# Constants later, Newton steps in another slot, and eight instead of twelve transfers an image, in a four-layer pre-activation kernel

## The chip, the cores and the metric

The kernel runs on one core of a Trainium2 chip. The metric is the device time of one execution in microseconds, lower is better. The engines go by the names of the profile: PE is TensorE's matrix product and PEld its weight load, DVE is VectorE, ACT is ScalarE, POOL is GpSimd, and SP is SyncE, which in this kernel does little but issue transfers (DMAs); its queue is shown as SPq. Each engine runs its own instructions in order; semaphores order the engines among each other.

## The reference

The input x has 4 images of 32x32 positions and 16 channels. Four layers each add a function of the normalized input:

```python
def _gn(v, G=8, eps=1e-5):                    # group norm over positions and channel pairs
    B_, H_, W_, C_ = v.shape
    g = v.reshape(B_, H_, W_, G, C_ // G)
    m = jnp.mean(g, axis=(1, 2, 4), keepdims=True)
    s = jnp.var(g, axis=(1, 2, 4), keepdims=True)
    return ((g - m) / jnp.sqrt(s + eps)).reshape(v.shape)

x = x + conv(_gn(x), L0_M, L0_W, L0_G)
x = x + conv(_gn(x), L1_M, L1_W, L1_G)
x = x + interval(_gn(x), W0, b0, W1, b1, W2, b2)
x = x + conv(_gn(x), L3_M, L3_Wp, L3_G)
```

In a convolution layer, with i, j an output position, c a channel and y, x an input position,

```python
first   = einsum('ijyx,byxc->bijc', M, v)
shifted = 3x3 convolution of v with the weights G[i, j], which differ for every i, j
diff    = relu(v - shifted)                   # one 32x32 plane for every b, i, j, c
second  = einsum('ijyx,bijyxc->bijc', W, diff)
return first - second
```

The interval layer takes a running maximum and a running minimum over all intervals (i, j), runs two steps of the form max over k of sigmoid(f[i,k] Wf + r[k,j] Wr + b), the second on the first's result, and ends with a linear map and a sigmoid.

Here 1024 output positions times 4 images times 16 channels each need a plane of 1024 values for every convolution layer, and this is nearly the whole work.

## The kernel before

**Tiling.** The 4 images are two groups g of 2 images b. Each convolution layer of each group is a phase, six in all: (g 0, layer 0), (g 1, layer 0), (g 0, layer 1) and so on; the kernel counts its convolution layers 0, 1, 2, the last being the reference's fourth. The interval layer belongs to the preparation of layer 2. A phase has 8 chunks t of 128 output positions, and a chunk has 32 steps, one for each output channel f and image b. So there are 6x8x32, 1536 steps. A step makes 128 planes in one pair of PSUM banks, of which there are four:

- first_part: PE multiplies the weights WL by ib and WU by ia (eight matmuls, L663 by way of products), and ACT scales the result in place (L699).
- second_part, issued one step later: PE adds the products of iyz and im9 (six matmuls), and DVE reads the pair, takes the minimum with 0, multiplies by the chunk's W (tile WT) and sums (L716, output junk). That frees the pair for the step four later.

The inputs ia, ib, iyz and im9 of a group are made in its preparation from the normalized images: split (L275 ff) separates each value into a high part and a rest (upper at L204 on DVE, the subtraction L281 on POOL, a scaling on ACT) and writes both to a tile temp; place (L291 ff) copies quarters of temp to other partitions of ia and ib by DMA, twelve an image (eight of 32x496 values for ia at L299, four of 32x2x512 for ib at L301); difference makes iyz. In the first chunk, which works with plain inputs for the first eight channels, temp is a part of the tile called first, and DVE does the subtraction.

**The weights' cycle.** A unit is the weights of 4 channels, used for 8 steps. The generator prep_parts (L221 ff) prepares the units one after the other; conv_layer advances it once a step, so a unit's preparation takes the 8 steps of another unit. Its slots, in order of steps:

- slot 1: DVE takes the high part, upper_w (L204);
- slot 2: ACT, W9 (L176);
- slot 3: ACT (L237) and POOL (L238, L239);
- slot 4: ACT (L241) and POOL (L242, two L244, two L246);
- slot 5: POOL subtracts the picked identity from the next unit's raw weights (L215);
- slot 6: nothing;
- slot 7: SP issues two transfers of parts to the other half of the partitions (L252) and the load of raw weights two units ahead (L111);
- slot 0: nothing.

**Everything else.** All other work of a phase (the preparation of the next group: norm, interval layer, image copies, split, place, and the product sum first_terms) is one long generator, behind(phase). conv_layer advances it after a step's matmuls have been issued: a yield of n waits n steps, a yield of IDLE waits for a slot in which the weights' cycle allows it (slots 1, 5, 6, 7, 0), a yield of CALM for one of slots 6, 7, 0. So a number in a yield decides in which slot of the cycle, and so between which instructions of POOL, DVE, ACT and SP, all the following work stands.

The order on each engine is the order in which the program issues, and nothing is reordered. SP issues all the transfers in that order too. The transfers of SP pass through eight semaphores in turn, so that a transfer is issued only when the one eight before it has landed.

**What the change and the prediction touch.** group_norm (L334 ff) sums over positions on DVE, transposes, sums again (by totals, with pauses of gap steps), makes mean, difference and squares on POOL (L366 ff), sums the squares in the same way, and takes the inverse root (inverse_root, three DVE instructions from L320 and thirteen POOL instructions, L326 to L331, three Newton steps) and the product with it (L376). The interval layer calls it with the name i0 or i1 and a gap of 2. constants (L462 ff) loads the interval layer's weights wv and bv, masks them and builds the small block matrices f0, f1, f2, r0, r1 by POOL products (L476). It is called once, in the first phase, in behind. step (L598 ff) is one of the interval layer's two steps; it ends in a sigmoid (L630) and four transfers of the hidden state s into the tile tables (L632), which left reads next on PE (L573). rest_of_start (L905 ff) prepares group 0 in the first chunk and ends in its norm, c00.

Of the kernel before, what the change touches and what calls it, by code (L numbers as in the profile page):

```python
# [8 lines left out]
F32 = mybir.dt.float32  # L9
F32R = mybir.dt.float32r  # L10
# [5 lines left out]
P = 128  # L16
B, H, C = 4, 32, 16
NG = 2
GB = B // NG
# [5 lines left out]
HW = H // 2  # L25
WP = HW + 2
PITCH = H * WP
NH = H * HW
RUN = (H - 1) * WP + HW
LAST = (H - 1) * HW  # L30
TAPS = ((0, 1, 2, 3), (6, 7, 4, 5))
TEMP = 2 * 2 * GB * NH
# [13 lines left out]
def net_kernel(ctx: ExitStack, tc: tile.TileContext, x, xq, xi, convs, iv_w, iv_b, out):  # L46
# [26 lines left out]
    nc = tc.nc  # L73
# [6 lines left out]
    big = ctx.enter_context(tc.tile_pool(name="big", bufs=1))  # L80
# [19 lines left out]
    CALM = -1  # L100
# [32 lines left out]
    first = big.tile([P, 8192], F32, tag="big", name="first")  # L133
    used = PLAIN * 3 * FU * P
# [60 lines left out]
    QUARTERS = [(slice(64 * h, 64 * h + 32), slice(64 * h + 32, 64 * h + 64)) for h in range(2)]  # L195
# [73 lines left out]
        halve_rest(units[u][3][:, at:to], raws[u][:, 2, at:to], low_p)  # L269

    def halves(temp, b):
        v = temp.rearrange("p (k s b n) -> p k s b n", k=2, s=2, b=GB)
        return v[:, 0, :, b], v[:, 1, :, b]

    def split(eng, g, b, temp, name, pause=IDLE):  # L275
# [14 lines left out]

    def place(g, b, temp):  # L291

        ty, tz = (v.bitcast(F32) for v in halves(temp, b))
        da, db = (v[g].bitcast(F32)[:, :, b] for v in (ia, ib))
        for h, (lo, hi) in enumerate(QUARTERS):
            for s in range(2):
                at = HW if s == h else 0
                for to, src in ((lo, ty), (hi, tz)):
                    nc.sync.dma_start(da[to, s, :LAST], src[lo, s, at : at + LAST])  # L299
            for to, src in ((lo, ty), (hi, tz)):  # L300
                nc.sync.dma_start(db[to], src[hi])  # L301
        yield 1


# [26 lines left out]
            nc.gpsimd.tensor_tensor(y, y, t, ALU.mult)  # L331
        return y

    def group_norm(g, name, dst, gap):  # L334


        def sums(src):
            nc.vector.tensor_reduce(
                part[:, : GC // 2], src.rearrange("p t (g s) -> p g t s", s=2), axis=AX.XY, op=ALU.add
            )  # L340

        def totals(name):

            turned = work.tile([P, 32], F32, tag="turned", name=f"turned_{name}")
            nc.vector.transpose(turned, part)
            by_quarter = work.tile([32, 4], F32, tag="by_quarter", name=f"by_quarter_{name}")
            for q in range(4):
                nc.vector.tensor_reduce(
                    by_quarter[:, q : q + 1], turned[32 * q : 32 * q + 32], axis=AX.X, op=ALU.add
                )  # L350
            yield gap
            total = work.tile([P, 32], F32, tag="total", name=f"total_{name}")
            for q in range(4):
                nc.vector.tensor_reduce(
                    total[32 * q : 32 * q + 32, 0:1], by_quarter, axis=AX.X, op=ALU.add
                )
            yield gap
            whole = work.tile([P, 32], F32, tag="whole", name=f"whole_{name}")
            nc.vector.transpose(whole, total[:, 0:1].to_broadcast([P, 32]))
            return whole[:, : GC // 2]  # L360

        sums(X[g])
        yield gap
        m = yield from totals(f"m{name}")
        mean = work.tile([P, GC // 2], F32, tag="mean", name=f"mean_{name}")
        nc.gpsimd.tensor_scalar_mul(mean, m, 1.0 / (2 * NP))  # L366
        xc = work.tile([P, NT, GC], F32, tag="xc", name=f"xc_{name}")
        nc.gpsimd.tensor_tensor(pair_view(xc), pair_view(X[g]), spread(mean), ALU.subtract)
        sq = work.tile([P, NT, GC], F32, tag="sq", name=f"sq_{name}")
        nc.gpsimd.tensor_tensor(sq, xc, xc, ALU.mult)  # L370
        yield 4
        sums(sq)
        yield gap
        v = yield from totals(f"v{name}")
        rstd = inverse_root(v, name)
        nc.gpsimd.tensor_tensor(pair_view(dst), pair_view(xc), spread(rstd), ALU.mult)  # L376
        yield 6

    xns = {}
    part = const.tile([P, 32], F32, name="part")  # L380
# [2 lines left out]
    def before_conv(g, layer):  # L383
        xn = work.tile([P, NT, GC], F32, tag="xn", bufs=2, name=f"xn_{g}_{layer}")
        xns[g] = xn
        yield from group_norm(g, f"c{g}{layer}", xn, 1 if layer == 2 else 4)

        nc.vector.transpose(  # L390
            xt[g][:, :, 1 : 1 + H], xn
        )
        inner = xs[g][:, :, WP : WP + H * WP].rearrange("p h (t r n) -> p h r t n", r=ROWS, n=WP)
        for r in range(ROWS):
            for h in range(2):
                nc.sync.dma_start(
                    inner[:, h, r], xt[g][GC * r : GC * (r + 1), :, HW * h : HW * h + WP]
                )
        yield 2
        xsv = xs[g].rearrange("(b c) h n -> c h b n", b=GB)  # L400
        for slot, row, tap in [
            (slot, row, tap) for slot in range(2) for row, tap in enumerate(TAPS[slot])
        ] + [(2, row, 8) for row in range(4)]:
            for h in range(2):
                off = tap // 3 * WP + tap % 3
                r0 = 64 * h + C * row
                nc.sync.dma_start(
                    raw[r0 : r0 + C, slot ^ h if slot < 2 else 2, :, :RUN], xsv[:, h, :, off : off + RUN]
                )
            yield 1  # L410
        yield 6 if layer == 2 else 12
        temp = big.tile([P, 8192], F32R, tag="big", name=f"temp_{g}{layer}")[:, :TEMP]
        for b in range(GB):
            yield from split(nc.gpsimd, g, b, temp, f"{g}{layer}")
            yield IDLE
            halve(image(im9[g][:, b], HW), image(raw[:, 2, b], WP), low_x)
            yield from place(g, b, temp)
            for s in range(2):
                difference(nc.gpsimd, g, b, s, temp)
            yield 1  # L420
            halve_rest(image(im9[g][:, b], HW), image(raw[:, 2, b], WP), low_x)
            yield 4
# [39 lines left out]
    def constants():  # L462
        nc.sync.dma_start(wv, iv_w)
        nc.sync.dma_start(bv, iv_b)
        mask2 = const.tile([P, GB], F32, name="mask2")
        nc.vector.tensor_reduce(
            mask2, ident.rearrange("p (s b c) -> p b s c", b=GB, c=C), axis=AX.XY, op=ALU.add
        )

        for at in (GC, 3 * GC):  # L470
            nc.gpsimd.tensor_scalar_mul(mask2[at : at + GC], mask2[at : at + GC], -1.0)
        yield 2

        def blocks(dst, k, mask, n, p0=0):
            p = dst.shape[0]
            nc.gpsimd.tensor_tensor(  # L476
                dst,
                wv[p0 : p0 + p, k, :].unsqueeze(1).to_broadcast([p, n, C]),
                mask[p0 : p0 + p].unsqueeze(2).to_broadcast([p, n, C]),
                ALU.mult,  # L480
            )

        nc.gpsimd.memset(rt, 0.0)
        yield 1


        for k, hidden, name in ((0, None, "f0"), (3, 2, "f1"), (6, 5, "f2")):
            n = 64 if hidden is None else 96
            t = const.tile([n, GB, C], F32, name=name)
            blocks(t[:64], k, mask2, GB)  # L490
            if hidden is not None:
                blocks(t[64:], hidden, mask2, GB, 64)
            iv[name] = t.rearrange("p k c -> p (k c)")
            yield 1
        for k, name in ((1, "r0"), (4, "r1")):
            t = const.tile([P, NQ * GB, C], F32, name=name)
            for q in range(NQ):
                blocks(t[:, q * GB : (q + 1) * GB, :], k, mask2, GB)
            iv[name] = t.rearrange("p k c -> p (k c)")
            yield 1  # L500
    def interval_layer(g):

        R = 2 * GC
        xi = ivp.tile([P, NT, GC], F32, tag="xi", name=f"xi_{g}")
        tables = big.tile([P, 8192], F32, tag="big", name=f"tables_{g}")
        n = H * H
        one, other, resets = (tables[:R, k * n : (k + 1) * n] for k in range(3))
        at = 3 * n
# [14 lines left out]
        yield 1  # L523
        nc.gpsimd.memset(r[:R, :, 0:1], 0.0)
        nc.gpsimd.memset(r[:R, H:], 0.0)
        yield from group_norm(g, f"i{g}", xi, 2)

        raw = one[:GC].rearrange("p (j t r) -> p r t j", j=H, r=ROWS)
        for row in range(ROWS):
# [68 lines left out]
        def step(name, ftp, bias):  # L598
# [26 lines left out]
                maxima(i, 0)  # L625
                yield 4
            maxima(QI - 2, 1)
            yield 3
            yield IDLE
            nc.scalar.activation(s, s, AF.Sigmoid, bias=bias)  # L630
            for q in range(NQ):
                nc.sync.dma_start(r[R:, QI * q : QI * (q + 1), :], s[GC * q : GC * (q + 1)])  # L632
            yield 4

        yield from right_side("r0", iv["r0"])
        ftp = left("l0", iv["f0"])
# [132 lines left out]
    def behind(phase):  # L769
        g, layer = phases[phase]  # L770
        if phase == 0:
            yield from rest_of_start()
            nc.sync.dma_start(X[1], x[1])
            zeros(1)
            yield 1
            yield from constants()
        if phase + 1 < len(phases):
            g1, layer1 = phases[phase + 1]
# [126 lines left out]
    def rest_of_start():  # L905
# [12 lines left out]
        halve_rest(image(im9[0][:, 1], HW), image(raw[:, 2, 1], WP), low_x)  # L918
        prep_plain_rest(1)
        yield 2  # L920
        temp = first.bitcast(F32R)[:, used : used + TEMP]
        for b in range(GB):
            yield from split(nc.vector, 0, b, temp, "00", 1)
            yield from place(0, b, temp)
# [4 lines left out]
        nc.vector.memset(part, 0.0)  # L929
        zeros(0)  # L930
        xns[0] = work.tile([P, NT, GC], F32, tag="xn", bufs=2, name="xn_00")
        yield from group_norm(0, "c00", xns[0], 4)

    parts = prep_parts()
    for phase in range(len(phases)):
# [80 lines left out]
```

## Time and profile before

| What | Value |
|---|---|
| Median of three runs | 2475.79 us (2475.51 to 2481.12) |
| The profiled execution | 2478.91 us |
| Its span (first to last instruction) | 2477.1 us |
| Granted TensorE clock | 1.000 of full speed |
| Matmuls of a step (L663), mean of one | 379 to 388 ns, 14 a step, pipelined |
| ACT on a step (L699) | 1008 ns |
| DVE on a step (L716) | 1224 ns, and 83 ns for the sum's read |
| POOL on a unit (L238, L239, L242; L244, L246 twice each; L215) | 1300, 1302, 1300; 609, 613; 1052 ns |
| Bytes moved | 366.92 MB, 148 GB/s |
| Transfers for ia and ib after the first preparation | 80 of 62 KB and 40 of 128 KB; landing after 5.6 and 4.4 us (medians) |
| Load of raw weights | 190 of 768 KB, 7.1 us (median) |
| SP's queue at an ia issue, waiting for a raw load to land | 26.1 us in all, 10 times |

In the groups of instructions, a row gives the source line, the engine, the operation, the tile written and the tiles read, the shape and the count; then the busy time, the mean of one, and the idle time of that engine just before these instructions with what ended most of it. In the timeline each row begins with its start and its duration in microseconds; a bracket at its end gives the engine's idle time before it and what released it. A table of waits sums such idle times by what was waited for. In the chain of waits, read from the last instruction back, each row is start, duration and what it was; PE's rows stand for matmuls, DMA's for the time from issue to landing.

An engine's idle time costs nothing unless it reaches the engine that sets the pace. A step that takes longer than the others shows as a late start of its first matmul in the timeline.

### The profile page before, as it was taken

How to read it: one execution, taken by the hardware profiler on the slowest of the kernel's cores; microseconds unless marked ns; L12 is line 12 of the kernel's file. 1: busy time of each engine (PE TensorE's matmuls, PEld its weight loads, DVE VectorE, ACT ScalarE, POOL GpSimd, SP SyncE). 2: the span in 40 equal slices, each digit the busy share in tenths (PEclk: the TensorE clock that was granted, in tenths of full speed). 3: DMA queues.
4: the chain of work that ended last, by engine and by line, in shares of the span. 5: the costliest groups of instructions: out<-in, count | busy, mean ns of one | idle time of the engine just before them, and what ended most of it. 6: DMA issues, size and time to landing. Idle time of an engine off the chain costs nothing. (4 is left out here: it accounts for less than half of the span.)

```text
span 2477.1 us, 58166 instructions
## 1 busy us (share of the span) xinstructions
PE 2457.9 (99%) x21906; PEld 2072.9 (84%) x21906; DVE 2077.0 (84%) x3637; ACT 1871.4 (76%) x2159; POOL 1589.7 (64%) x1857
## 2 busy tenths in 40 slices
PE   8999999999999999999999999999999999999999
PEld 5998888888888888888888898888889888888887
DVE  9888878888888888878888888888888888788887
ACT  3778767787777778767777777777777787677776
POOL 4767545676565667555567776776777675555552
PEclk9999999999999999999999999999999999999999
DMA  6457654475444467644454454674445476554442
GB/s 198 128 156 191 188 144 134 131 195 149 135 142 137 137 168 194 190 112 136 137 145 129 126 142 132 174 171 130 129 135 141 119 197 186 154 148 137 137 137 54
DMA packets 97674, 366.92 MB, mean 148 GB/s; under 512 B 26480, under 2 KB 31472, under 8 KB 97392
## 3 DMA queue, kind: packets, MB, share of 16 engines
q1 hardware_dynamic: 96832, 362.79, 53.5%
q8 instruction: 172, 2.82, 0.5%
q14 instruction: 110, 0.90, 0.1%
q10 hardware_dynamic: 432, 0.39, 0.0%
q0 software_dynamic: 128, 0.02, 0.0%
HBM read 199.78 MB, written 1.02 MB: 81 GB/s over the span
## 5 line engine op out<-in xcount | busy, mean ns | idle before, releaser
L716 DVE SCALAR_TENSOR_TENSOR junk<-pc,WT 128x1024 f32<-128x1024 f32 x1536 | 1879.6, 1224 | 353.5 <-PE pc L663 303.8
L699 ACT ACTIVATE pc<-pc 128x1024 f32<-128x1024 f32 x1520 | 1532.2, 1008 | 563.8 <-PE pc L663 530.4
L663 PE MATMUL pc<-ib,parts 64*128 64x512 f32 x6080 | 950.2, 388 | 4.3 <-DVE junk L716 3.0
L663 PE MATMUL pc<-iyz,parts 64*128 64x512 f32 x6080 | 947.2, 387 | 2.3 <-ACT pc L699 1.6
L663 PE MATMUL pc<-ia,parts 64*128 64x496 f32 x6080 | 924.8, 379 | 0.0
L663 PEld LDWEIGHTS pc<-ib,parts 64*128 64x128 f32 x6080 | 582.4, 184 | 109.8 <-DVE junk L716 9.6
L663 PEld LDWEIGHTS pc<-ia,parts 64*128 64x128 f32 x6080 | 585.4, 184 | 106.0
L663 PEld LDWEIGHTS pc<-iyz,parts 64*128 64x128 f32 x6080 | 583.5, 184 | 92.6 <-ACT pc L699 7.3
L663 PE MATMUL pc<-im,W 64*128 64x496 f32 x3072 | 603.2, 384 | 0.0
L238 POOL TENSOR_TENSOR parts<-raw,upper_w 128x512 fp32r<-128x512 f32 x190 | 247.0, 1300 | 497.6 <-DVE upper_w L204 413.1
L663 PEld LDWEIGHTS pc<-im,W 64*128 64x128 f32 x3072 | 296.6, 184 | 56.9 <-issue 3.4
L244 POOL CAST parts<-parts 32x512 fp32r<-32x512 f32 x380 | 231.6, 609 | 39.3 <-ACT parts L241 20.8
L242 POOL TENSOR_TENSOR parts<-parts 128x512 fp32r<-128x512 f32 x190 | 247.0, 1300 | 1.6 <-ACT parts L237 1.5
L246 POOL CAST parts<-upper_w 32x512 fp32r<-32x512 f32 x380 | 233.1, 613 | 22.8
L239 POOL TENSOR_TENSOR W<-W,raw 128x512 fp32r<-128x512 f32 x190 | 247.4, 1302 | 0.4 <-ACT W L176 0.3
L215 POOL TENSOR_TENSOR raw<-raw,ident 128x512 f32<-128x512 f32 x190 | 199.8, 1052 | 73.7 <-DMA raw<-in_g 45.8
L176 ACT ACTIVATE W<-raw,low_w 128x512 fp32r<-128x512 f32 x190 | 136.2, 717 | 1.7 <-DMA raw<-in_g 1.6
L716 DVE DVE_READ_ACCUMULATOR junk<-pc,WT 128x1 f32 x1536 | 127.9, 83 | 0.0
L237 ACT ACTIVATE parts<-upper_w 128x512 fp32r<-128x512 f32 x190 | 118.9, 626 | 7.7 <-DVE upper_w L204 7.5
L241 ACT CAST parts<-upper_w 128x512 fp32r<-128x512 f32 x190 | 116.4, 613 | 0.0
L731 POOL TENSOR_SCALAR acc<-acc 128x32 f32<-128x32 f32 x40 | 15.6, 391 | 136.8 <-DVE junk L716 134.7
L204 DVE TENSOR_SCALAR upper_w<-raw 128x512 int32<-128x512 int32 x190 | 82.4, 433 | 19.0 <-POOL raw L215 18.6
(152 smaller groups left out, 470.4 us busy)
## 6 DMA issues: line engine op xcount, KB each, us to landing
raw<-in_g SPq DMA_DIRECT2D x190, 768.0 KB, 7.1
parts<-parts SPq DMA_DIRECT2D x380, 384.0 KB, 5.0
WT<-in_w SPq DMA_DIRECT2D x48, 512.0 KB, 4.7
MT<-in_mt SPq DMA_DIRECT2D x24, 512.0 KB, 7.3
raw<-xs SPq DMA_DIRECT2D x120, 71.8 KB, 4.1
ib<-temp SPq DMA_DIRECT2D x40, 128.0 KB, 4.4
ia<-temp SPq DMA_DIRECT2D x80, 62.0 KB, 5.6
ib<-first SPq DMA_DIRECT2D x8, 128.0 KB, 2.4
```

Of the source, the lines that this page charges most:

```text
L176: nc.scalar.activation(dst, src, AF.Copy, scale=mask[:, 1:2])
L215: eng.tensor_tensor(raws[u][:, s, at:to], raws[u][:, s, at:to], pick[s][:, f0 + at : f0 + to].unsqueeze(2).to_broadcast([P, to - at, P]), ...
L237: nc.scalar.activation(WD, high, AF.Copy, scale=-EPS)
L238: nc.gpsimd.tensor_tensor(WL, w8, high, ALU.subtract)
L239: nc.gpsimd.tensor_tensor(W9, W9.bitcast(F32), src[:, 2], ALU.add)
L241: nc.scalar.copy(WU, high)
L242: nc.gpsimd.tensor_tensor(WD, WD.bitcast(F32), WL.bitcast(F32), ALU.add)
L244: nc.gpsimd.tensor_copy(WU[hi], WL[lo].bitcast(F32))
L246: nc.gpsimd.tensor_copy(WL[lo], high[hi])
L663: nc.tensor.matmul(ps[:, h, at : at + n], lhsT=w[r], rhs=v[r] if n == NH else v[r][:, :n], start=first and k == 0, stop=k == len(pairs) - ...
L699: nc.scalar.activation(ps, ps, AF.Copy, scale=1.0 + EPS)
L716: nc.vector.scalar_tensor_tensor(junk, ps.rearrange("p h n -> p (h n)"), 0.0, chunks[n], op0=ALU.min, op1=ALU.mult, accum_out=accs[phase][ ...
```

## The change

Five edits, most of them in the pauses of behind.

1. place sends ib first (four transfers as before), then ia in four transfers of 32x2x496 instead of eight of 32x496: both halves s of a quarter lie in temp at a fixed distance, 16 values (half an image row) more or less than the distance of the two planes, and one access pattern with that pitch covers them. To form the pattern, temp is no longer cut to TEMP columns when it is made, and halves cuts it.
2. group_norm gets a pause before inverse_root and the number of steps after it as arguments. The norm of group 0 in the first chunk (c00) gets a CALM pause there.
3. The interval norm (i0, i1) gets gap 1 instead of 2, the CALM pause, and 4 steps behind it instead of 6.
4. constants starts 6 steps after the zeros instead of 1, has 9 steps instead of 2 after the loads, 2 instead of 1 after clearing rt, and one step for each of the four blocks of r0 and r1. What comes after it in the first phase starts 24 steps later (three units).
5. In step, the wait before the sigmoid is 2 steps instead of 3, and the wait after its transfers is 5 instead of 4.

```diff
     def halves(temp, b):
-        v = temp.rearrange("p (k s b n) -> p k s b n", k=2, s=2, b=GB)
+        v = temp[:, :TEMP].rearrange("p (k s b n) -> p k s b n", k=2, s=2, b=GB)
         return v[:, 0, :, b], v[:, 1, :, b]
...
     def place(g, b, temp):
 
-        ty, tz = (v.bitcast(F32) for v in halves(temp, b))
+        parts = halves(temp.bitcast(F32)[:, :TEMP], b)
         da, db = (v[g].bitcast(F32)[:, :, b] for v in (ia, ib))
+        for lo, hi in QUARTERS:
+            for to, src in zip((lo, hi), parts):
+                nc.sync.dma_start(db[to], src[hi])
         for h, (lo, hi) in enumerate(QUARTERS):
-            for s in range(2):
-                at = HW if s == h else 0
-                for to, src in ((lo, ty), (hi, tz)):
-                    nc.sync.dma_start(da[to, s, :LAST], src[lo, s, at : at + LAST])
-            for to, src in ((lo, ty), (hi, tz)):
-                nc.sync.dma_start(db[to], src[hi])
+            for k, to in enumerate((lo, hi)):
+                at = (2 * k * GB + b) * NH + HW * (1 - h)
+                pitch = GB * NH + HW * (2 * h - 1)
+                src = temp.bitcast(F32)[lo, at : at + 2 * pitch].rearrange("p (s n) -> p s n", s=2)
+                nc.sync.dma_start(da[to, :, :LAST], src[:, :, :LAST])
         yield 1
...
-    def group_norm(g, name, dst, gap):
+    def group_norm(g, name, dst, gap, pause=None, behind=6):
...
         sums(sq)
         yield gap
         v = yield from totals(f"v{name}")
+        if pause is not None:
+            yield pause
         rstd = inverse_root(v, name)
         nc.gpsimd.tensor_tensor(pair_view(dst), pair_view(xc), spread(rstd), ALU.mult)
-        yield 6
+        yield behind
...
-        temp = big.tile([P, 8192], F32R, tag="big", name=f"temp_{g}{layer}")[:, :TEMP]
+        temp = big.tile([P, 8192], F32R, tag="big", name=f"temp_{g}{layer}")
...
         for at in (GC, 3 * GC):
             nc.gpsimd.tensor_scalar_mul(mask2[at : at + GC], mask2[at : at + GC], -1.0)
-        yield 2
+        yield 9
...
         nc.gpsimd.memset(rt, 0.0)
-        yield 1
+        yield 2
...
             for q in range(NQ):
                 blocks(t[:, q * GB : (q + 1) * GB, :], k, mask2, GB)
+                yield 1
             iv[name] = t.rearrange("p k c -> p (k c)")
-            yield 1
...
-        yield from group_norm(g, f"i{g}", xi, 2)
+        yield from group_norm(g, f"i{g}", xi, 1, CALM, 4)
...
             maxima(QI - 2, 1)
-            yield 3
+            yield 2
             yield IDLE
             nc.scalar.activation(s, s, AF.Sigmoid, bias=bias)
             for q in range(NQ):
                 nc.sync.dma_start(r[R:, QI * q : QI * (q + 1), :], s[GC * q : GC * (q + 1)])
-            yield 4
+            yield 5
...
             zeros(1)
-            yield 1
+            yield 6
             yield from constants()
...
-        temp = first.bitcast(F32R)[:, used : used + TEMP]
+        temp = first.bitcast(F32R)[:, used:]
...
-        yield from group_norm(0, "c00", xns[0], 4)
+        yield from group_norm(0, "c00", xns[0], 4, CALM)
```

## The prediction

> **What bounds the kernel now.** I began with the page's engine row, the clock row and the two costliest groups.
>
> ```profile
> PE 2457.9 (99%) x21906; PEld 2072.9 (84%) x21906; DVE 2077.0 (84%) x3637; ACT 1871.4 (76%) x2159; POOL 1589.7 (64%) x1857
> ...
> PEclk9999999999999999999999999999999999999999
> ...
> L716 DVE SCALAR_TENSOR_TENSOR junk<-pc,WT 128x1024 f32<-128x1024 f32 x1536 | 1879.6, 1224 | 353.5 <-PE pc L663 303.8
> ```
>
> PE is busy 99% of the span at full clock, and DVE's main instruction mostly waits for PE. So TensorE's products set the pace, and the change removes none of them. In the timeline the first product of consecutive steps starts at 794.65, 796.22, 797.79 us: a step is 1.567 us, and 1536 of them are the time. The periods above that pace, summed over all steps after the twentieth, are 46.2 us. Only these can be won, and a stall counts only if it reaches a PE row. I therefore listed the long periods in the timeline and looked for those whose cause the edit touches. Three numbers serve below. A PSUM buffer comes back when DVE has read it; in steady steps DVE ends 1.65 us before PE needs that buffer, so **DVE may be 1.65 us late for nothing**, and it catches up 0.2 us a step (1.567 less 1.23+0.08 for L716, less its other work). A weight unit takes 8 steps, 12.54 us; POOL's part of it, from L238 to the end of L215, takes 7.6 us and starts right after upper_w (L204), so with some 0.5 us of starts **POOL may be 4.4 us late** before the next L204 waits. L204 stands in order in front of L716, which is how POOL's lateness reaches PE.
>
> **The change part by part.** Times over pace are sums of periods less 1.567.
>
> *Interval norm (L326 to L376, twice).*
>
> ```profile
> 1276.82 1.29 POOL L238 TENSOR_TENSOR parts<-raw,upper_w 128x512 fp32r<-128x512 f32 x1
> ...
> 1284.45 0.43 DVE L204 TENSOR_SCALAR upper_w<-raw 128x512 int32<-128x512 int32 x1 [2.49 <-POOL raw L215]
> ...
> 1286.07 0.73 PE L663 MATMUL pc<-ib,parts 64*128 64x512 f32 x4 [0.80 <-DVE junk L716]
> ```
>
> The Newton steps sit in slot 1 of the unit, ahead of L238; they last 1272.12 to 1276.86, so L238 starts at 1276.82 instead of about 1270.3, 6.5 late against 4.4. L204 waits 2.49, PE 0.80, and DVE needs many steps to recover: from 1272 to 1303 the periods stand 2.01 us over pace, and 2.01 again for the second group (1684 to 1715). The edit puts the Newton steps three steps earlier, in slot 6, where POOL is free: 1272.1−3×1.567 is 1267.4 to 1272.1, L238 follows at about 1272.3, its L215 ends at 1279.9, and L204 is due at 1282: 2 us to spare. What stays is ACT's 1.06 us multiplication in that stretch (L533, 1295.16), for which I leave 0.3. Gain 1.7 twice, **3.4**. The price is crowding: pauses of 1 instead of 2 put DVE's reductions and transposes into consecutive steps. No row shows this norm so. The nearest is the layer-2 convolution norm, which has pauses of 1: at 1550 DVE was 1.89 late, 0.07 short of the limit, and the steps 1554 to 1558 lost 0.36. By adding the reductions to the DVE rows of this stretch I get at most 1.45, below 1.65. I take 0, between 0 and 0.4 each. Below nothing is excluded, as no DVE work goes. The mean's three POOL instructions fall behind the copies L246, and their unit's L215 ends at 1256.1 for an L204 at 1256.9: hidden, by 0.8 plus DVE's 1.65.
>
> *First norm and constants.*
>
> ```profile
> 108.19 0.23 POOL L476 TENSOR_TENSOR f<-wv,mask 64x32 f32<-64x32 f32 x1 [2.46 <-DMA wv<-in_iv_w]
> ...
> 115.74 0.50 PE L663 MATMUL pc<-ib,parts 64*128 64x512 f32 x2 [1.06 <-DVE junk L716]
> ```
>
> The first norm's Newton steps (87.81 to 92.55) delay L238 in the same way; L204 waits 1.80 at 100.14, and 95 to 108 is 0.68 over pace. They move five steps, to slot 6, the place argued above: gain 0.68. Then the first constant block waits 2.46 on POOL for a load of wv, with L242 to L215 queued behind it; L204 waits 2.41, PE 1.06, and 108 to 131 is 1.48 over pace. The edit loads wv ten steps later and uses it another eleven steps (17 us) after, where an issue at 103.20 landed at 108.12; and the thirteen small blocks (0.23 to 0.26 each) come one or two a step. Gain 1.48. Everything behind them (mask, X[1]'s load, the norm of image group 1, its transfers, the MT loads, the first product sum from step 195 to 219) moves by 24 steps, three whole units, so each instruction and DMA meets the same slot of a unit and the same free queue as before. The first terms' matmuls only run later (7.27 us over pace before and after). The two mask products now stand before L238 behind a DVE reduction: L238 is 3.65 late of 4.4, so 0, or 0.3 if that sum is off. Together **2.2**.
>
> *Eight transfers an image (L291 ff).*
>
> ```profile
> 1625.18 5.42 SPq L299 DMA_DIRECT2D ia<-temp  x4
> 1630.64 1.29 SPq L301 DMA_DIRECT2D ib<-temp  x2
> 1632.12 1.16 SPq L252 DMA_DIRECT2D parts<-parts  x2
> 1633.69 0.82 SPq L111 DMA_DIRECT2D raw<-in_g  x1
> ...
> 1643.95 1.04 POOL L215 TENSOR_TENSOR raw<-raw,ident 128x512 f32<-128x512 f32 x1 [7.36 <-DMA raw<-in_g]
> ```
>
> SP issues everything in order, and each transfer waits for the one eight before it. The eighth after the raw of 1617.60 (landed 1628.34) is issued at 1628.36, and four more follow it before parts and raw can go. So this raw goes out at 1633.69 and lands at 1643.82; POOL waits 7.36 for it and PE, at 1645.59, 1.21; 1638 to 1653 is 1.94 over pace. With eight transfers the eighth is the image's last, so parts follow at about 1628.95 instead of 1632.12: 3.2 us earlier, more than PE's whole stall. Gain 1.94. In the first chunk it is the same: the blocked eighth is issued at 46.11, the last ib at 48.63 lands at 51.01, and PE waits 0.96 for it (51.14); the period is 1.25 long. With ib first, its four transfers land by 47.6 and ia by about 48.5, before PE asks at 50.18. Gain 1.25. The other four preparations show no PE stall at this place, so the earlier issue is worth nothing there. Together **3.2**.
>
> A rule speaks against this. The Trainium skill, "DMA: Bandwidth & Descriptors", section "Issuing engines are not separate DMA queues", says that the time a sequencer takes to initiate a DMA is usually small beside the DMA. The bytes stay 1008 KB an image (8×62+4×128 before, 4×124+4×128 after), so by the rule alone this part is worth 0 and my sum drops to 6.9. The trace has twelve issues at 0.54 to 0.63 an image, seven us, against a landing of 5.6 (ia, the page's median), and a queue behind them: I go by the rows.
>
> The part adds a wait: image 1's first split (L281, POOL) writes a tile that image 0's ia transfers now read whole, so it waits for them. Queued behind it are L238 to L215. In the five preparations after the first, the transfer at the same count landed at 542.35, 943.97 and so on, and L281 started at 545.73, 947.23, 1615.56, 2027.35: margins 3.4, 3.3, 2.2 and 2.0 us. I cost it at 0.
>
> *Sigmoid and its four transfers one step earlier.*
>
> ```profile
> 1935.62 5.67 DMA tables<-s_b
> 1941.29 0.14 issue
> 1941.43 1.07 PE ps_l L573 x8
> ```
>
> This is the chain of waits: PE waits 0.73 here and 0.61 at 1529 for the hidden state's transfers. One step is 1.567, so they land about 1.0 us before PE asks. The matmuls remain. The four issues (2.65 us) now go ahead of parts and raw, which leave 4.3 us later (1520.53 to about 1524.8); that raw would land at about 1533.4 and L215 takes it at 1534.36: hidden by 1 us, else 0.3. Gain 0.61+0.73, **1.3**.
>
> **Sum.** 3.4+2.2+3.2+1.3 is 10.1 us against the profiled execution, 2478.91 (span 2477.1 and 1.81 around it): 2468.8. The median of the runs shown is 3.1 lower, with runs from 2475.51 to 2481.12, so some stalls of the profile are not in every run. The instruction-timed ones (norms and constants, 5.56) I take in full, of the transfer-timed ones (4.53) some seven tenths: 8.8. **Forecast 2467.0**, chance 0.60.
>
> **Rivals.**
>
> 1. *Transfer stalls are taken over* (0.20). Where PE no longer waits for ib, s_b or this raw, the next of that queue is late. For it: every raw around images takes 9 to 10 us. Against: the eighth transfer then is the last before parts. Only norms and constants pay: 2475.8−5.6 is 2470.2.
> 2. *DVE crowding* (0.12). Pauses of 1 push DVE beyond 1.65 twice. For it: the row at 1550. Then D's 3.4 goes and 0.36 to 1 is paid each time: 8.8−3.4−0.8 is 4.6, 2471.2.
> 3. *Slower: image 1's split waits on POOL* (0.08). Place: L281, five preparations. If ia's landing took the 10.1 us of raw in this stretch instead of 2 to 2.5, at 1611.93 it would end at 1622.0, 6.3 after L281's start. Decisive from 2.0 (margin) plus 1.8 (POOL's slack left after L281's 2.58) plus 1.65: some 5.5 us late; with weight loads as long as that, DVE's recovery at 0.2 a step doubles the direct 0.8 to 3 us, five times 3.4 against 8.8: 2484. Against it: merged ia is 124 KB, near ib's 128 KB, which lands in 4.4 (page).
>
> **Numbers.** What a measurement can tell from no change is 0.3%, 7.4 us, so below 2468.4 is faster. The forecast's 0.60 and a third of rival 1 make 0.66; the rest of rivals 1 and 2 are within, 0.28; slower is most of rival 3, 0.06. The range: low 2463.5 is the lowest run less the whole 10.1 and 1.9 more, one stall of 1638's size saved elsewhere; high 2473.5 takes in rivals 1 and 2 with the unknown costs (0.4 twice, 0.3 twice) and leaves out rival 3.
>
> **What will show it.** L204's waits at POOL L215 near 100, 114, 1284 and 1696 gone; no PE idle at 51, 1286, 1529, 1645, 1941; SP's raw near 1630; L281 of image 1 without an idle before it. Idle before L238 for a DMA, or DVE's L716 more than 1.65 us behind near 1250 to 1275, would prove me wrong.

## The result and the profile after

| | Before | After |
|---|---|---|
| Median, six runs each | 2477.49 us (2475.51 to 2482.97) | 2469.16 us (2468.21 to 2470.02) |
| The profiled execution, and its span | 2478.91, 2477.1 | 2470.02, 2468.3 |
| Sum of the periods over pace after step twenty | 46.20 us | 37.70 us |

The ratio is 0.9963, with a 95% interval of 0.995 to 0.9976: 8.3 us less by the medians, 8.9 between the two profiled executions. From here on lines of place, group_norm and what follows are 2 to 4 higher than before: L328 is the Newton steps' first row, L380 the product after them, L480 a constant block, L667 the products, L720 DVE on a step.

First the pages: DVE's upper_w of the kernel before, and then of the changed kernel the engines, the clock and the same row.

```profile
L204 DVE TENSOR_SCALAR upper_w<-raw 128x512 int32<-128x512 int32 x190 | 82.4, 433 | 19.0 <-POOL raw L215 18.6
```

```profile
PE 2454.2 (99%) x21906; PEld 2039.1 (83%) x21906; DVE 2077.4 (84%) x3637; ACT 1871.7 (76%) x2159; POOL 1587.7 (64%) x1857
...
PEclk9999999999999999999999999999999999999999
...
L204 DVE TENSOR_SCALAR upper_w<-raw 128x512 int32<-128x512 int32 x190 | 82.4, 434 | 8.1 <-POOL raw L215 7.6
```

PE still sets the pace at full clock, and nothing of its work is gone. DVE's waiting for POOL's L215 fell by 11 us. The timeline of the changed kernel at the first interval norm (start, duration):

```profile
1268.67 0.67 POOL L380 TENSOR_TENSOR xi<-xc_i,root_y_i 128x256 f32<-128x256 f32 x1
1269.31 1.29 POOL L238 TENSOR_TENSOR parts<-raw,upper_w 128x512 fp32r<-128x512 f32 x1
...
1275.87 1.04 POOL L215 TENSOR_TENSOR raw<-raw,ident 128x512 f32<-128x512 f32 x1
...
1280.14 0.43 DVE L204 TENSOR_SCALAR upper_w<-raw 128x512 int32<-128x512 int32 x1
```

L215 ends 3.2 us before L204, where it had been the cause of a 2.49 us wait. The constants, in the timeline:

```profile
131.37 1.30 POOL L480 TENSOR_TENSOR f<-wv,mask 64x32 f32<-64x32 f32 x5
```

No bracket: the wait of 2.46 us for wv is gone. And SP's queue where the second image of group 0 is placed for layer 2:

```profile
1611.86 1.26 SPq L111 DMA_DIRECT2D raw<-in_g  x1
1613.21 3.48 SPq L297 DMA_DIRECT2D ib<-temp  x4
1616.73 6.18 SPq L303 DMA_DIRECT2D ia<-temp  x4
1624.14 2.27 SPq L252 DMA_DIRECT2D parts<-parts  x2
1626.52 0.54 SPq L111 DMA_DIRECT2D raw<-in_g  x1
...
1632.67 1.04 POOL L215 TENSOR_TENSOR raw<-raw,ident 128x512 f32<-128x512 f32 x1
```

The raw weights land before L215 needs them. The sigmoid's transfers, at the place where the chain of waits stood before:

```profile
1926.08 2.44 SPq L636 DMA_DIRECT2D tables<-s_b  x4
1928.63 1.17 SPq L252 DMA_DIRECT2D parts<-parts  x2
...
1933.03 0.66 PE L577 MATMUL ps_l<-tables,f 96*32 96x264 f32 x8
```

PE's left product has no idle time before it now.

Not everything went down. The chain of waits of the changed kernel leaves PE once in chunk 30, in a place where before had no loss:

```profile
1563.23 9.25 DMA raw<-in_g
1572.49 0.30 SPq L411
...
1576.53 7.24 DMA parts<-parts
1583.77 0.04 issue
1583.81 6.35 PE pc L667 x48
```

A raw load took 9.25 us. The eighth transfer after it, one of the image's copies, could not be issued before it had landed, the parts transfers stood behind those copies, and PE waited for parts.

The periods over pace by place, in us, of both kernels (chunks of 32 steps; half a chunk where it says so):

| Place | What the change does there | Before | After | Predicted change |
|---|---|---|---|---|
| chunk 0, second half | eight transfers | 1.25 | 0.47 | -1.25 |
| chunk 1, second half | first norm, constants | 2.03 | 0.00 | -2.16 |
| chunks 3 (second half) and 4 | moved by 24 steps | 0.41 | 0.86 | 0 |
| chunks 24 and 25, middle | interval norm | 2.00 | 0.30 | -1.7 |
| chunks 27 and 35, end | first sigmoid of a layer | 4.00 | 3.54 | 0 |
| chunks 29 and 37 | second sigmoid | 4.54 | 2.99 | -1.34 |
| chunk 30, second half | nothing | 0.00 | 1.44 | 0 |
| chunk 31, second half | eight transfers | 1.94 | 0.00 | -1.94 |
| chunks 32 and 33, middle | interval norm | 2.01 | 0.30 | -1.7 |

### The profile page after: what moved, and what is told of

Its sections match the earlier page's. It is cut to its first block, busy times and chain, and to the rows that moved or that the text cites. A ratio compares the mean times of both kernels' runs of the same rounds, so it can differ in the third digit from the quotient of the medians.

```text
span 2468.3 us, 58094 instructions
## 1 busy us (share of the span) xinstructions
PE 2454.2 (99%) x21906; PEld 2039.1 (83%) x21906; DVE 2077.4 (84%) x3637; ACT 1871.7 (76%) x2159; POOL 1587.7 (64%) x1857
## 4 chain that ended last, share of the span: by engine, by line
PE 97%; DMA 1%; ACT 1%; issue 0%; DVE 0%; SPq 0%; ACTq 0%; DVEq 0%
PE pc L667 95%; PE pf L443 1%; DMA raw<-in_g 1%; ACT pc L703 1%; DMA first<-in_g 0%; DMA parts<-parts 0%; DVE junk L720 0%; ACT temp L285 0%; PE ps_l L577 0%; SPq L400 0%; SPq L411 0%; PE ps_r L592 0%; SPq L252 0%; DVE W L179 0%; ACT im L176 0%
## 5 line engine op out<-in xcount | busy, mean ns | idle before, releaser
L720 DVE SCALAR_TENSOR_TENSOR junk<-pc,WT 128x1024 f32<-128x1024 f32 x1536 | 1879.7, 1224 | 355.6 <-PE pc L667 305.1
L667 PE MATMUL pc<-ib,parts 64*128 64x512 f32 x6080 | 944.4, 387 | 0.7 <-DMA parts<-parts 0.7
L667 PE MATMUL pc<-iyz,parts 64*128 64x512 f32 x6080 | 942.0, 387 | 1.3 <-ACT pc L703 0.7
L667 PE MATMUL pc<-ia,parts 64*128 64x496 f32 x6080 | 919.9, 379 | 0.0
L667 PEld LDWEIGHTS pc<-ia,parts 64*128 64x128 f32 x6080 | 575.3, 184 | 115.9
L667 PEld LDWEIGHTS pc<-ib,parts 64*128 64x128 f32 x6080 | 573.5, 184 | 113.2 <-issue 4.9
L667 PEld LDWEIGHTS pc<-iyz,parts 64*128 64x128 f32 x6080 | 574.1, 184 | 100.4 <-ACT pc L703 5.6
L667 PE MATMUL pc<-im,W 64*128 64x496 f32 x3072 | 598.4, 384 | 0.0
L238 POOL TENSOR_TENSOR parts<-raw,upper_w 128x512 fp32r<-128x512 f32 x190 | 247.2, 1301 | 525.1 <-DVE upper_w L204 443.9
L667 PEld LDWEIGHTS pc<-im,W 64*128 64x128 f32 x3072 | 291.6, 184 | 61.9 <-issue 3.4
L246 POOL CAST parts<-upper_w 32x512 fp32r<-32x512 f32 x380 | 233.1, 613 | 22.8
L215 POOL TENSOR_TENSOR raw<-raw,ident 128x512 f32<-128x512 f32 x190 | 198.0, 1042 | 57.1 <-DMA raw<-in_g 24.5
L176 ACT ACTIVATE W<-raw,low_w 128x512 fp32r<-128x512 f32 x190 | 136.2, 717 | 0.3 <-DMA raw<-in_g 0.2
L720 DVE DVE_READ_ACCUMULATOR junk<-pc,WT 128x1 f32 x1536 | 128.0, 83 | 0.0
L204 DVE TENSOR_SCALAR upper_w<-raw 128x512 int32<-128x512 int32 x190 | 82.4, 434 | 8.1 <-POOL raw L215 7.6
```

The costliest lines, as they stand in the source:

```text
L176: nc.scalar.activation(dst, src, AF.Copy, scale=mask[:, 1:2])
L215: eng.tensor_tensor(raws[u][:, s, at:to], raws[u][:, s, at:to], pick[s][:, f0 + at : f0 + to].unsqueeze(2).to_broadcast([P, to - at, P]), ...
L238: nc.gpsimd.tensor_tensor(WL, w8, high, ALU.subtract)
L246: nc.gpsimd.tensor_copy(WL[lo], high[hi])
L667: nc.tensor.matmul(ps[:, h, at : at + n], lhsT=w[r], rhs=v[r] if n == NH else v[r][:, :n], start=first and k == 0, stop=k == len(pairs) - ...
L720: nc.vector.scalar_tensor_tensor(junk, ps.rearrange("p h n -> p (h n)"), 0.0, chunks[n], op0=ALU.min, op1=ALU.mult, accum_out=accs[phase][ ...
```

## The experiments

Four kernels have one part of the change each, on top of the kernel before. Then come kernels that leave one part out of the changed kernel, and repeats. "Over pace" in the expectations and below is the same sum as in this table.

**One part at a time.** The edits are the hunks of the change shown above, no others: t_only has place with halves and temp, i_only the interval norm's call, c_only the pause in c00 with constants, s_only the two pauses in step.

> The kernel before with the eight transfers an image alone. If the parts are independent, as the prediction has it: the first chunk's stall falls from 1.25 us over pace to about 0.5 and the one at chunk 31 (1.94) to 0, everything else as before, so 2.7 to 3.2 us less. If the transfers' stalls only move to the next of the queue: 0 to 1 us less, with a new wait of POOL for raw weights in another preparation, as the changed kernel's profile shows one at chunk 30 (1.44 over pace).

> The kernel before with the interval norm's edit alone. Slot theory: the periods from chunk 24 step 16 to chunk 25 step 31, and the same in chunks 32 and 33, fall from 2.0 to 0.3 us over pace each, 3.4 us less in all, nothing else moves. If DVE crowding in the tighter norm gave part of it back, DVE would reach its limit of 1.65 us near 1250 to 1270 and the gain be 2 us or less.

> The kernel before with the pause in the first norm and the later constants alone. Prediction: chunk 1's second half goes from 2.0 us over pace to 0, all later work of the first phase only 24 steps later, so 2.0 us less. If the later preparation of image group 1 meets other transfers than before, chunks 3 and 4 lose 0.4 to 0.5 us more than before, as they do in the changed kernel (0.2 and 0.3).

> The kernel before with the sigmoid and its four transfers one step earlier alone. Prediction: chunks 29 and 37 lose 0.7 and 0.8 us less; the first of the two steps (chunks 27 and 35), which the prediction did not count, loses 0.25 less each; together 1.3 to 2.0 us less. If the four transfers in front of parts and raw cost something, chunks 29 to 30 lose more than before, and the 1.44 us of chunk 30 in the changed kernel shows here.

Before stood at 2477.86 (57 runs, 2475.10 to 2483.01).

| Kernel | Median (runs) | Ratio, 95% interval | Chunk 0 | Chunk 1 | 24+25 | 32+33 | 29 | 37 | 30 | 31 |
|---|---|---|---|---|---|---|---|---|---|---|
| t_only | 2476.61 (13) | 0.9995, 0.9987 to 1.0003 | 0.46 | 1.72 | 2.04 | 2.01 | 2.31 | 2.31 | 0.49 | 0.00 |
| i_only | 2475.37 (21) | 0.9992, 0.9986 to 0.9999 | 0.45 | 1.87 | 0.26 | 0.30 | 2.22 | 2.07 | 0.00 | 0.39 |
| c_only | 2477.13 (21) | 0.9996, 0.9990 to 1.0003 | 0.73 | 0.00 | 1.99 | 2.00 | 2.42 | 2.33 | 0.00 | 0.10 |
| s_only | 2476.61 (13) | 0.9993, 0.9985 to 1.0002 | 0.75 | 1.90 | 2.32 | 2.05 | 1.47 | 1.49 | 0.62 | 1.14 |

By the profile each part does what was predicted at its own place: the interval norm takes 1.7 twice, the constants 2.0, the sigmoid 0.75 and 0.85. By medians t_only is only 1.25 us below before, and not the 2.7 to 3.2 that its expectation had. And look at chunks 0 and 31. The three kernels that keep the twelve transfers have 0.45 to 0.75 and 0.10 to 1.14 there, and not the 1.25 and 1.94 that I had read in the one profile of before. And s_only has two losses at places that its edit doesn't touch, 2.05 in chunk 3 and 1.39 in the second half of chunk 39. The latter is taken up below. In its table of waits for chunk 3 (time in us, times, longest) the cause is a raw load:

```profile
POOL raw L215 <- DMA raw<-in_g: 7.3, 1, 7.3
...
DVE upper_w L204 <- POOL raw L215: 2.4, 1, 2.4
```

So some stalls belong to one execution. The timed runs of these kernels spread over 3.6 to 8 us, for which such stalls are the likely reason (a run without a profile doesn't show it), and no single part is clear by itself beyond i_only.

**One part left out, and repeats.** a_no_t has place, halves and temp of before. a_slot1 keeps the gap of 1 and puts the Newton steps back in slot 1, so it tells the slot from the gap:

```diff
-        yield from group_norm(g, f"i{g}", xi, 1, CALM, 4)
+        yield from group_norm(g, f"i{g}", xi, 1, 6, 6)
```

a_no_s has the pauses of before in step. a_again and a_third are the changed kernel, b_again the kernel before.

> The changed kernel once more. Median 2469 us, 8 to 9 less than before. The 1.44 us over pace at chunk 30 came from a raw load that took 9.94 us: if that is the chance of one execution, this profile has 0 to 0.6 there and may have a stall of that kind elsewhere; if the change causes it, 1.2 to 1.6 again. Single parts gave 1.25, 2.5, 0.7 and 1.25 us by medians, 5.7 in all: if the parts are additive, this median falls towards 2472.

> The changed kernel with the twelve transfers an image of before. If the transfers are worth what they gave alone, the median is 1.2 us above the changed kernel, 2470.4. If the prediction's 3.2 holds where the other stalls are gone, 2472.4. In the profile, chunk 0's second half between 0.45 and 1.25 us over pace, chunk 31 between 0 and 1.94, since both came out differently in single executions of kernels that have these transfers unchanged.

> The changed kernel with the interval norm's Newton steps back in slot 1 (a pause of 6 steps in place of CALM, 6 steps behind as before), the gap still 1. Slot theory: chunks 24 to 25 and 32 to 33 are again about 2.0 us over pace each, so 3.4 us more than the changed kernel, 2472.6; upper_w waits for L215 about 2.5 us near 1280. If the shorter gaps are what helped, they stay at 0.3 and the median at 2469.2.

> The kernel before once more, for a second profile. Stalls timed by instructions are as in the first (chunk 1 2.0, chunks 24 to 25 2.0, chunks 32 to 33 2.0 us over pace); those timed by raw loads differ: chunk 31 between 0 and 1.9, chunk 0 between 0.45 and 1.25, and others may be there that the first did not have.

> The changed kernel with the sigmoid's pauses of before (3 and 4 steps). Chunks 29 and 37 are again 2.2 to 3.0 and 2.3 us over pace, chunks 27 and 35 2.0 each: 1.8 to 2.8 us above the changed kernel on this chip by the profile. The part alone gave 1.25 by medians; if the parts are less than additive, 1.2.

> The changed kernel on the same chip, to compare the other two with: median 2469 to 2470 us, chunk 30 between 0 and 1.4 us over pace, chunk 4 0.6 to 1.0.

The first four ran on one chip, where before took 2480.06 (9 runs), the last two on another, where it took 2479.12 (11 runs).

| Kernel | Median (runs) | Ratio, 95% interval | Chunk 0 | 3+4 | 24+25 | 32+33 | 29 | 37 | 30 | 31 | 17, and 39 (second half) |
|---|---|---|---|---|---|---|---|---|---|---|---|
| a_again | 2470.00 (5) | 0.9958, 0.9946 to 0.9971 | 0.53 | 0.94 | 0.29 | 0.29 | 1.49 | 1.47 | 0.00 | 0.00 | 0, 0 |
| a_no_t | 2471.56 (5) | 0.9964, 0.9952 to 0.9977 | 0.66 | 1.19 | 0.29 | 0.29 | 1.47 | 1.48 | 0.00 | 0.00 | 0.92, 0.65 |
| a_slot1 | 2471.13 (5) | 0.9964, 0.9950 to 0.9978 | 0.46 | 0.97 | 1.51 | 1.24 | 1.46 | 1.49 | 0.58 | 0.00 | 0.08, 0 |
| b_again | 2478.04 (1) | | 0.68 | 0.42 | 2.30 | 1.93 | 3.02 | 2.39 | 0.93 | 0.90 | 0, 0 |
| a_third | 2468.80 (5) | 0.9954, 0.9942 to 0.9967 | 0.25 | 0.56 | 0.29 | 0.29 | 1.46 | 1.49 | 0.51 | 0.00 | 0.43, 0 |
| a_no_s | 2471.45 (5) | 0.9964, 0.9951 to 0.9978 | 0.22 | 1.29 | 0.29 | 0.26 | 3.35 | 2.27 | 1.00 | 0.00 | 0.28, 0 |

*The slot and the gap.* a_slot1 was expected at 2.0 twice and has 1.51 and 1.24. Its timeline:

```profile
1279.41 1.04 POOL L215 TENSOR_TENSOR raw<-raw,ident 128x512 f32<-128x512 f32 x1
1280.48 0.43 DVE L204 TENSOR_SCALAR upper_w<-raw 128x512 int32<-128x512 int32 x1 [1.72 <-POOL raw L215]
```

L204 waits 1.72 instead of 2.49. So of the 1.7 that each norm gained, the slot (with the shorter pause behind it) is worth 1.22 and 0.95 (1.51 and 1.24 less 0.29); the rest, some 0.5 to 0.8, comes with the gap, in which alone a_slot1 differs from before in this stretch. (The kernels with the old norm differ among themselves by up to 0.33 at one of these places, so the split is rough.) A shorter gap puts DVE's reductions further ahead of the Newton steps; that this is how it helps was not tried by itself. The medians of a_slot1 and a_again, 1.1 apart, agree in sign.

*The transfers in chunk 31, and in chunk 39.* Here is the landing of the late raw load from the traces, counted from the first product of step 1000, and the loss:

```
kernel     transfers  issued  landed  time   over pace
a_no_t        12       19.27   28.15   8.88    0.00
c_only        12       19.71   28.94   9.23    0.10
i_only        12       20.36   29.18   8.82    0.39
b_again       12       20.01   29.68   9.67    0.90
s_only        12       20.33   29.91   9.58    1.14
before        12       20.57   30.70  10.13    1.94
after          8       17.50   22.66   5.16    0.00
a_slot1        8       15.54   22.62   7.08    0.00
```

With twelve transfers the loss is the landing less 28.8, to within 0.04 once it is late enough to show well (29.18 onward), and the landing differs by 2.5 us between executions. With eight, it is issued about 3 us earlier (in a_slot1 4.5) and lands after 5.2 to 5.4 us in five profiles and 7.1 in a_slot1, instead of 8.8 to 10.1. In all six it has landed by 22.8, so it has some 6 us to spare. This stall is in none of the profiles with the edit; but it is worth 0.75 on the mean of the six executions, not 1.94.

Chunk 39 is the same place of the other image group, 256 steps later, and there the same rule holds. Counted from step 1256, the load landed at 30.18 in s_only and at 29.45 in a_no_t; less 28.8 that is 1.38 and 0.65, and the losses are 1.39 and 0.65. What POOL and DVE waited for in s_only (us in all, times, longest):

```profile
POOL raw L215 <- DMA raw<-in_g: 7.9, 2, 6.6
...
DVE upper_w L204 <- POOL raw L215: 3.5, 2, 2.8
```

In the other four executions with twelve transfers it landed at 25.9 to 28.7, and nothing was lost; with eight it landed at 22.8 or before. So s_only's loss in chunk 39 is a stall of the twelve transfers too, which happened not to be in the one profile of before: 0.34 on the mean of the six. The edit changes the order (ib first) and the number of transfers together, and no run separates the two.

*Chunk 30.* The changed kernel's 1.44 is 0.00 in a_again and 0.51 in a_third, and the kernel before has 0.00 and 0.93 in its two profiles: it differs between executions of one program. It goes with how late SP's queue is there. Counted from step 976, the raw load that is issued there (at 1577.23 in the changed kernel) landed at 15.45 or before where nothing was lost, and at 15.73 to 17.19 where 0.49 to 1.44 was. The second parts transfer, issued just ahead of it, on which PE waits in the chain of waits above, landed at 12.58 or before, and at 12.98 to 13.79. The two are late together, so these runs don't tell which of them costs how much. Nor do they settle whether fewer transfers make this stall more frequent: two of the six executions with twelve have it, and five of the six with eight.

*Chunks 3 and 4.* All seven profiles with the later constants have 0.14 to 0.28 in chunk 3 and 0.41 to 1.14 in chunk 4. Without that edit it is 0.00 and 0.41 to 0.45, but for s_only's stall in chunk 3. So moving the first phase's work by 24 steps costs some 0.5 us on the mean; what causes it, no run shows.

*The sum.* Means over the profiles give: for the transfers 1.4 (0.75 in chunk 31, 0.34 in chunk 39 and 0.35 in chunk 0, where the six executions with twelve transfers average 0.75, six with eight 0.40); for the interval norms 3.5; for the first norm and the constants 2.0 less the 0.5 of chunks 3 and 4. The sigmoids give 2.0 between the first two profiles, but chunk 29 too is uneven with the old pauses: 2.2 to 3.0 in before, b_again, t_only, i_only and c_only, and 3.35 in a_no_s, which is above what I had expected there. With the new pauses it is 1.46 to 1.49 in all six profiles so far, so the mean gain of the sigmoids is 2.4 (1.1 in chunk 29, 0.8 in chunk 37, 0.5 in chunks 27 and 35). That is 8.8 us, against 8.3 in the first comparison and 10.1 and 10.3 in the two repeats. By medians, the four parts alone give 1.25, 2.5, 0.7 and 1.25, only 5.7; left out, the transfers cost 1.6 and the sigmoid 2.7, close to the profiles' 1.4 and 2.4. The singles' intervals contain the profiles' values, each of them; whether a part really is worth more in the company of the others, these runs don't settle.

**An earlier raw load.** Since late raw loads cause what is left of the uneven stalls, I tried to issue them a step earlier, in slot 6, where nothing else of the cycle is. a_raw6 moves the load alone, ahead of the parts transfers, a_both6 moves the parts transfers and the load behind them:

```diff
             yield (IDLE,)
+            load_raw(u + RAWS)                      # a_raw6
             yield (IDLE, CALM)
             for h in range(2):
...
-            load_raw(u + RAWS)                      # a_raw6
             yield (IDLE, CALM)
...
             yield (IDLE,)
-            yield (IDLE, CALM)                      # a_both6
             for h in range(2):
...
             yield (IDLE, CALM)
+            yield (IDLE, CALM)                      # a_both6
```

> The changed kernel with the load of raw weights issued one step earlier, in slot 6, ahead of the two parts transfers instead of behind them. If what is left of the uneven stalls (chunk 4 0.67 to 1.01 us over pace where before has 0.41, chunk 30 0 to 1.44, chunks 17 and 39 now and then) comes from raw loads that land late and from parts that queue behind transfers waiting for such a load, they go: chunk 4 0.4, chunk 30 0, and the median is 0.5 to 1 us below the changed kernel on this chip. If parts behind a 768 KB load land too late, PE waits for parts at the start of units and the median is 1 us or more above it.

> The changed kernel with the two parts transfers and the load of raw weights behind them issued one step earlier, in slot 6, in their old order. The kernel with the raw load alone in front lost 3.15 and 2.14 us over pace where PE waited for parts. If it is the order that costs, these two stalls are absent here, chunk 4 is 0.4 and chunk 30 0 to 0.5 us over pace, and the median is 2468 to 2469.5 us, the same as the changed kernel or up to 1 us less. If the earlier place costs (SP then waits for POOL's copies with the image's transfers queued behind, and the four transfers of the sigmoid come behind parts and raw again), chunks 29 and 37 rise from 1.5 to about 2.2 and the median to 2470 or more.

a_raw6 took 2474.75 (7 runs, 2469.21 to 2476.52), 5.95 more than a_third on the same chip. One step of chunk 9 starts 3.15 late, where the others lose nothing, and chunk 4 has 3.00 over pace instead of 0.41 to 1.14. Its timeline of SP and PE:

```profile
495.14 0.43 SPq L111 DMA_DIRECT2D raw<-in_g  x1
...
496.66 1.10 SPq L253 DMA_DIRECT2D parts<-parts  x2
...
508.88 0.50 PE L667 MATMUL pc<-ib,parts 64*128 64x512 f32 x1 [2.55 <-DMA parts<-parts]
```

The second parts transfer, issued at 497.18 behind the raw load, landed at 508.84, after 11.7 us; in the changed kernel's profile the one at the same place took 5.9 (494.00 to 499.94). The median time of a raw load fell from 7.1 to 4.3, and PE paid for it at the start of a unit.

a_both6, in the old order, took 2477.54 (13 runs, 2476.74 to 2478.44; ratio to before on its chip 0.9991, 0.9983 to 1.0): so what the change had brought is lost, but for 1.9 us that these runs hardly tell from nothing. The two stalls of a_raw6 are absent (chunk 9 0.00, chunk 4 0.50), and the raw load's median is 7.2 again, so these go with the order of the transfers. But chunks 30 and 38 have 3.9 over pace each, chunk 29 2.97, chunk 37 2.44. What the queue of SP waited for near chunk 30:

```profile
SPq L251 <- POOL parts L246: 10.1, 2, 8.9
```

Here SP comes to the parts transfer 8.9 us before POOL has made the data (POOL has the Newton steps of the layer-2 norm ahead of that unit's L238), and the image's transfers stand behind it in the queue; twelve of them then go ahead of the next parts (1573.04 to 1579.02), on which PE waits. Both guesses of mine failed, and in both the second theory of the expectation was right in kind; the losses were larger than it had named. No version here beats the changed kernel.

## Why the prediction was right

- **Bound and method**: right. PE kept its 99%, and the gain is the sum of stalls that reached PE. 8.8 was forecast, 8.3 measured in the first comparison and 10.1 and 10.3 in the repeats; 2469.16 lies 2.2 above the forecast, of which 1.7 is that before itself came out at 2477.49 over more runs. That the total fits so well is in part luck: the transfers and the constants were put too high and the sigmoids too low, and these errors nearly cancel.
- **Interval norm, 3.4**: 3.41 between the profiles. The place in slot 6 was right; I had given all of it to the slot, and about a third is the gap's. DVE was at most 1.1 us late in this stretch (near 1260), not beyond the 1.65: rival 2 is out. By the same measure DVE near 1556, the nearest case I had, was 1.58 late and not 1.89; 0.07 short of the limit was right.
- **First norm and constants, 2.2**: chunk 1 is at 0.00 in every profile that has the edit, and at 1.72 to 2.03 in those without. But I had put the move by 24 steps at 0, and it costs some 0.5.
- **Transfers, 3.2 (2.2 after the discount)**: the mechanism was right, the size was not. The eighth transfer is the last of an image, the raw load went out 3.1 us earlier (parts 3.9), and the stall in chunk 31 is gone. The terms 1.25 and 1.94 were one execution's; the runs give 0.35 and 0.75, and 0.34 in chunk 39, where I had seen no stall to win. I had discounted transfer-timed stalls by three tenths for that reason, and it should have been more than half for these. In chunk 0 I had also taken the whole stall as won. PE no longer waits for ib there, but one step later it waits for ACT's scaling, and that step starts 0.53 late in the changed kernel:

```profile
52.33 0.30 PEld L667 LDWEIGHTS pc<-iyz,parts 64*128 64x128 f32 x4 [0.65 <-ACT pc L703]
```

Neither side had the size. The Trainium skill's rule ("DMA: Bandwidth & Descriptors", section "Issuing engines are not separate DMA queues"), that initiating is usually small beside the DMA, holds here for a single issue, 0.6 us of 5.6. But the 1.4 of this part lies between the 0 that I had drawn from it and the 3.2 of the rows. What the rows had right is that the load behind an image's transfers goes out earlier with eight of them than with twelve, by 3.2 us on the mean of six and six executions.

- **The wait added at L281**: I had margins of 2.0 to 3.4 us. In the four preparations for which I had these, they came out as 2.7, 2.2, none (a wait of 0.43) and 0.25, because an image's last ia transfer landed 2.9 to 5.0 us after its issue and not after 2 to 2.5. Rival 3 did not happen, but it was nearer than I said.
- **Sigmoid, 1.3**: 1.55 between the profiles, 1.9 on the mean of six and six executions, and 0.5 more in chunks 27 and 35, which I had missed. PE does not wait for transfers at that first step of the layer, in any of these profiles. There the sigmoid stood directly ahead of L176 on ACT, so that the scaling came late, and PE's next weights waited for it; in the changed kernel a scaling stands between the two, and this wait is absent. The kernel before, in the timeline:

```profile
1436.56 0.51 ACT L630 ACTIVATE s_a<-s_a,bv 128x264 f32<-128x264 f32 x1
...
1436.97 0.71 ACT L176 ACTIVATE W<-raw,low_w 128x512 fp32r<-128x512 f32 x1
...
1437.59 1.01 ACT L699 ACTIVATE pc<-pc 128x1024 f32<-128x1024 f32 x1
...
1438.65 0.30 PEld L663 LDWEIGHTS pc<-iyz,parts 64*128 64x128 f32 x4 [0.33 <-ACT pc L699]
```

- **Rival 1** (the next of the queue is late): the stall in chunk 30 is of this kind. Before has it too in one of two profiles, so the change is not its only cause; whether it makes it more frequent stays open.

## What to carry to other kernels

Before a stall is counted as gain, see whether it is timed by instructions or by transfers: the first kind was there in every profile of a kernel that has it, to within some 0.3 us, the second differed by up to 2 us at one place, so one profile is one draw of it. With queues in order, an instruction that waits should come late enough that its data is there: here a transfer in a quiet slot was worse than the same transfer one slot later. And small pieces of vector work belong in the part of the cycle in which the engine they delay has nothing due.

## What the runs showed that I had not expected

The time of one 768 KB load at one place, with the same twelve transfers ahead of it, differs by 1.3 us between executions (8.8 to 10.1), and the loss follows its landing one to one once the 28.8 us are up, in chunk 31 and again in chunk 39. With four issues fewer ahead of it, the same load takes 5.2 to 7.1: its time depends on the transfers around it, by more than 4 us at the same size. How much of this is those ahead of it, and how much the next unit's parts and raw load, which are issued 23 to 25 us after step 1000 while a late load is still under way, no run separates. And the order of two kinds of transfers, 768 KB ahead of two of 384 KB or behind them, moved the median of the former from 7.1 to 4.3 us and gave one of the latter 11.7.
